# Masked attention with a residual on one core: the last outputs reordered, the short row group in four blocks, the seventh batch finished earlier

## The chip, the core and the metric

The kernel runs on one core of a Trainium2 chip. The engines of that core are TensorE (called PE in the profile, with its weight loads as PEld), VectorE (DVE), ScalarE (ACT), GpSimd (POOL) and SyncE (SP), and sixteen DMA engines move data between the memory outside (DRAM) and the core. Each engine works through its own list of instructions in order and waits at an instruction until what that one needs is there. The metric is the device time of one execution in microseconds; a lower one is better.

## The reference

`x` has the shape (8, 512, 1024): 8 batches, 512 features, 1024 tokens. For each batch the reference computes

```python
xt = jnp.transpose(x, (0, 2, 1))
q = xt @ Wq.T                                   # queries, keys and values are the same
qh = q.reshape(B, T, 8, 64).transpose(0, 2, 1, 3)
scores = jnp.einsum('bhqd,bhkd->bhqk', qh, qh) / 8
logits = (scores * cmask + (1 - cmask) * -1e30) * rmask
ctx = jnp.einsum('bhqk,bhkd->bhqd', jax.nn.softmax(logits, -1), qh)
x = x + jnp.transpose(ctx.transpose(...).reshape(B, T, D) @ Wo.T, (0, 2, 1))
```

The mask is 0 or 1 per token, about half and half. A masked token is no key for the others, and as a query it attends to all tokens evenly. So the kernel computes attention for the kept tokens alone, and one mean for all the rest.

## The kernel before, in words

For each batch the kept tokens are gathered to the front: 544 columns for the inputs at hand (`NK`), of which the last is the mean of the queries over all tokens and stands for the masked ones. These columns make five groups (`sizes`): four of 128, numbers 0 to 3, and a short one of 32, number 4, which the code calls `LAST`. The 512 features are four pairs of heads. A pair of a batch is the unit of the main loop in `late`: 32 pairs, four for each of the eight batches. I write (b, p) for the pair p of batch b; the last batch is 7 and the last pair (7, 3).

Each pair runs through five slots, one for each group c of keys. In a slot the kernel emits, in this order: the score products of the group (`scores`, L662, and L676 for the short group) and their exponentials on ACT (L685); the products of exponentials and values (`weigh_behind`, L709) of an earlier group; and then the tasks that `plan` has put into this slot. A task has a rank: those under 5 come first, then `contexts` of a pair that is due, then those from 5 up. The order is written out by hand and nothing is rearranged later, so a slot's place decides what stands ahead of what on each engine. PSUM has two buffers under the tag "t" for all the side products, two under "av", and two double ones for the scores.

What happens to a pair afterwards:

- `end_values` (L738) copies the weighted values to `cT`. `inverses` (L769 to L776, DVE) inverts the sums of the exponentials. For all but the last two pairs `invert` sends the inverses through DRAM to spread them over the partitions (`rb`). For the last two `spread` (L756) does it with 20 small products on PE and two copies on ACT (L763). In the kernel before, the spread for (7, 2) stands in slot 0 of (7, 3), right behind `inverses`.
- `contexts` (L803 to L812, DVE) finishes the inverses of the short group (`sum_last`), multiplies `cT` by `rb` and puts the mean into the last column.
- When all four pairs of a batch are done, `output` (L834) multiplies a group's contexts by the output weights, ACT copies the result (L841), and POOL's queue stores it to a table in DRAM, `od` (L846). The short group's output is computed in four blocks of 32 partitions and 128 columns.
- `load_rows` (L902, SP's queue) loads the rows of x, `fetch` (L943, POOL) gathers the rows of `od` and adds them in the DMA, `finish_blocks` (L913, DVE) turns 128 tokens of the result back to features by tokens in the tile `whole`, and `issue_stores` (L922, SP's queue) writes `whole` out, four stores for each half of batch 6 and of batch 5.

For the last batch there is another end. `begin_output` (L861) computes a group's output over the first three pairs and ACT copies this partial result (L869, `pa`); it runs in the slots of (7, 3). Behind the loop stand the last values' products, `spread` for (7, 3), the partial output of the short group, `sum_last`, `end_values_last` (L746, the contexts of the last pair straight from PSUM), and `end_output` (L876) for the groups 0, 4, 1, 2, 3: the product over the last pair, the sum with the partial result on DVE (L884) and the store on SP's queue (L885). Then DVE turns the last two token blocks of batch 6, SP's queue stores the second half of its `whole`, `fetch_last` (L934, POOL) gathers the rows of batch 7 by eight indirect DMAs, and `finish_tokens` turns each on PE (L960), adds x on DVE (L961) and stores on ACT's queue (L962). The first gather reads groups 0 and 4 alone, and each further gather one more group.

One more rule sets waits on PE: `note` remembers the first read of a PSUM buffer in a slot, and `open_slot` and `pass_gate` make the first value product (or crossed projection) of the next slot wait for it. Where no read was noted, it waits for the first exponential of the slot's own scores.

## Time and profile before

| | us |
|---|---|
| device time, median of 3 runs | 677.13 (675.56 to 678.43) |
| device time of the profiled execution | 679.92 |
| its span, first to last instruction | 677.9 |
| PE busy | 621.4 (92% of the span) |
| DVE busy | 362.0 (53%) |
| ACT busy | 360.5 (53%) |
| POOL busy | 184.1 (27%) |
| mean granted PE clock | 0.963 |

A row of the timeline gives the start, the duration, the engine, the line of the kernel, the operation, the tile written and the tile read, their shapes, how many records were merged (x16), and in brackets the idle time of the engine just before and what ended it. In the chain of work that ended last, a row is start, duration, what. In a table of stretches, each engine has its busy time, then come the granted PE clock, the share of the DMA engines that was busy, and GB/s. A product of 32-bit numbers leaves two records. SPq, ACTq and POOLq are the instructions that issue DMAs. The place of the tasks in this execution: (7, 0) runs from about 556 us, (7, 1) from 574, (7, 2) from 595, (7, 3) from 613, and the loop ends at about 639.

### The profile page before, as it was taken

Reading aid. Unit: us, or ns where it says so; the run is one execution under the profiler, and the core shown is the slowest. Engines: PE = TensorE matmul, PEld = TensorE weight load, DVE = VectorE, ACT = ScalarE, POOL = GpSimd, SP = SyncE. Lnnn points to the kernel's source line nnn. Section 1 sums busy time; section 2 is a strip of 40 time slices with the busy share of each in tenths; the row PEclk is TensorE's granted clock in tenths of the full one; section 3 lists DMA queues with packets and bytes.
Section 4 is the critical chain, followed back from the end, with each engine's and each line's share of the span. In section 5 each row is a group of like instructions: output and inputs, shape, how many; then the busy total and the mean of one; then the engine's idle time right before and its main releaser. Section 6 shows DMA issues by size and latency. Waiting matters only on the chain.

```text
span 677.9 us, 21834 instructions
## 1 busy us (share of the span) xinstructions
PE 621.4 (92%) x9056; PEld 413.2 (61%) x9056; DVE 362.0 (53%) x1113; ACT 360.5 (53%) x1010; POOL 184.1 (27%) x203
## 2 busy tenths in 40 slices
PE   6578989999999979999999999999999999998953
PEld 5345657677666656667666666676666655554422
DVE  6325885654564555555664566457645535234252
ACT  5127667656655645556656665656655445544300
POOL 4600221100134212341224304331334207006240
PEclk9688999999999989999999999999999999998985
DMA  8533663533366865696769777785857468744666
GB/s 277 170 122 98 197 192 89 165 97 113 103 197 141 215 185 154 205 252 164 198 227 247 169 187 247 195 196 150 233 135 144 130 212 154 211 146 78 128 197 190
DMA packets 98544, 117.10 MB, mean 173 GB/s; under 512 B 11785, under 2 KB 65625, under 8 KB 98426
## 3 DMA queue, kind: packets, MB, share of 16 engines
q1 hardware_dynamic: 77976, 75.71, 37.4%
q0 software_dynamic: 16224, 37.71, 24.4%
q10 hardware_dynamic: 4226, 2.10, 1.1%
q8 instruction: 75, 1.23, 0.8%
q14 instruction: 43, 0.35, 0.2%
HBM read 72.81 MB, written 42.67 MB: 170 GB/s over the span
## 4 chain that ended last, share of the span: by engine, by line
PE 76%; DMA 8%; DVE 7%; ACT 3%; SPq 2%; issue 2%; POOL 1%; DVEq 0%; ACTq 0%; POOLq 0%
PE s L662 17%; PE av L709 17%; PE pq L542 15%; PE po L834 15%; PE v L579 3%; DMA x<-in_x_dram 2%; PE pa L861 2%; PE xc L485 2%; DVE len L601 1%; ACT e L685 1%; DVE xc L488 1%; PE top L615 1%; PE s L676 1%; DMA rb<-row 1%; DMA g<-od,origin 1%
## 5 line engine op out<-in xcount | busy, mean ns | idle before, releaser
L685 ACT ACTIVATE e<-s,bias 128x544 f32<-128x544 f32 x256 | 180.3, 709 | 89.1 <-PE s L662 88.7
L709 PE MATMUL av<-e,v 64*64 64x272 f32 x2048 | 162.5, 398 | 7.9 <-ACT el L685 4.3
L662 PE MATMUL s<-qT 64*64 64x272 f32 x2048 | 155.8, 399 | 0.0
L542 PE MATMUL pq<-xc,wqT 64*64 64x272 f32 (+1 forms) x1984 | 127.5, 390 | 0.2 <-DVE xc L488 0.2
L709 PEld LDWEIGHTS av<-e,v 64*64 64x64 f32 x2048 | 85.5, 134 | 52.6 <-ACT cT L738 8.5
L834 PE MATMUL po<-woT,cT 128*128 128x256 f32 (+2 forms) x624 | 114.7, 363 | 0.0
L662 PEld LDWEIGHTS s<-qT 64*64 64x64 f32 x2048 | 82.3, 134 | 36.2 <-issue 6.9
L542 PEld LDWEIGHTS pq<-xc,wqT 64*64 64x64 f32 x1984 | 79.2, 134 | 37.5 <-issue 0.8
L943 POOL DMA_INDIRECT g<-od,origin x48 | 75.8, 1578 | 84.8 <-DMA g<-xd 60.5
L834 PEld LDWEIGHTS po<-woT,cT 128*128 128x128 f32 (+1 forms) x624 | 79.2, 164 | 28.8 <-issue 15.1
L846 POOL DMA_DIRECT2D od<-oc x56 | 31.3, 562 | 202.6 <-ACT oc L841 200.4
L472 POOL DMA_INDIRECT xin<-xd,source x40 | 39.8, 995 | 130.8 <-DMA row<-rt 71.8
L488 DVE COPY xc<-xc 128x512 f32<-128x512 f32 (+1 forms) x37 | 22.0, 613 | 61.4 <-PE xc L485 61.4
L559 DVE COPY qT<-pq 128x272 f32<-128x272 f32 x32 | 14.1, 439 | 70.2 <-PE pq L542 65.2
L841 ACT COPY oc<-po 128x256 f32<-128x256 f32 (+2 forms) x57 | 21.7, 382 | 55.8 <-PE po L834 55.8
L685 ACT ACTIVATION_READ_ACCUMULATOR e<-s,bias 128x1 f32 x256 | 50.2, 196 | 0.0
L588 DVE COPY v<-v 128x320 f32<-128x320 f32 x64 | 28.3, 483 | 34.3 <-PE v L579 34.3
L913 DVE STREAM_TRANSPOSE whole<-g 128x512 f32<-128x512 f32 x56 | 37.4, 687 | 13.8 <-DMA g<-od,origin 9.1
L601 DVE TENSOR_REDUCE len<-sq 128x10 f32<-128x640 f32 x32 | 26.1, 814 | 30.5 <-ACT sq L595 30.4
L738 ACT COPY cT<-av 128x272 f32<-128x272 f32 x62 | 21.1, 389 | 37.6 <-PE av L709 37.5
L425 ACT ACTIVATE junka<-x 128x512 f32<-128x512 f32 x64 | 40.2, 628 | 0.7
L462 DVE TENSOR_SCALAR_CACHE_REDUCE junk<-rank,key 128x1024 f32<-128x1024 f32 (+4 forms) x40 | 39.8, 996 | 0.0
(156 smaller groups left out, 633.4 us busy)
## 6 DMA issues: line engine op xcount, KB each, us to landing
xd<-xt SPq DMA_DIRECT2D x120, 128.0 KB
x<-in_x_dram SPq DMA_DIRECT2D x56, 256.0 KB
g<-xd SPq DMA_DIRECT2D x48, 256.0 KB
out_dram<-whole SPq DMA_DIRECT2D x20, 512.0 KB
rb<-row SPq DMA_DIRECT2D x60, 160.0 KB
od<-oc POOLq DMA_DIRECT2D x28, 256.0 KB
out_dram<-whole SPq DMA_DIRECT2D x16, 256.0 KB
rank<-ranks SPq DMA_DIRECT2D x7, 512.0 KB
```

The costliest lines, as they stand in the source:

```text
L425: nc.scalar.activation(junk, xs[b][r][:, d, :], AF.Copy, accum_out=xbars[b][:, d, r : r + 1])
L462: nc.vector.tensor_scalar(junk[:, :n], rank[:, i * P :], key[:, col], 0.0, ALU.is_le, ALU.add, accum_out=found[:, col])
L472: nc.gpsimd.indirect_dma_start(out=xin[:n, :], out_offset=None, in_=rows_of_x[b], in_offset=bass.IndirectOffsetOnAxis(ap=searches[b][2][:n ...
L542: mm = nc.tensor.matmul(pqs[pair][hf][heads[h], :n], wqT[rows, d, at : at + DK], xcs[b][rows, d, hf * KH : hf * KH + n], start=(not cross ...
L601: nc.vector.tensor_reduce(lengths, sq.rearrange("p c (h d) -> p (c h) d", h=2), axis=AX.X, op=ALU.add,)
L662: nc.tensor.matmul(s[h][to, hf, :KH], qT[heads[h], at : at + DK], qT[heads[h], hf * KH : (hf + 1) * KH], start=True, stop=True,)
L685: act = nc.scalar.activation(e[:, h], of[h], AF.Exp, bias=biases[pair][:, c : c + 1], scale=SCALE, accum_out=acc[:, h, c : c + 1],)
L709: mm = nc.tensor.matmul(avs[pair][hf][heads[h], :KH], v[rows, c, heads[h]], e[rows, h, hf, :] if c < LAST else e[rows, h, :], start=(c == ...
L834: nc.tensor.matmul(po[j * n : (j + 1) * n, cols], cTs[b, pr][:, i * P : i * P + n], woT[:, pr, j * w + cols.start : j * w + cols.stop], st ...
L846: nc.gpsimd.dma_start(od[places[i], j * w : (j + 1) * w], oc[j * n : (j + 1) * n, :w])
L913: nc.vector.transpose(whole.rearrange("p (d a) n -> p a d n", a=A)[:, :, :, i * Q : (i + 1) * Q], gs.pop((b, i)).rearrange("p (a d f) -> p ...
L943: nc.gpsimd.indirect_dma_start(out=gs[b, i], out_offset=None, in_=ods[b], in_offset=bass.IndirectOffsetOnAxis(ap=origin[:, b, i : i + 1] i ...
```

## The change

Five edits, all of them in the last two batches:

1. Batch 6's outputs of the groups 3 and 4 move from slot 3 of (7, 2) to (7, 1): the short one to slot 3, the other to slot 4. Its gathers move from slots (7, 2, 4) to (7, 3, 2) to slots (7, 2, 1) to (7, 3, 1), and its eight turns (`finish_blocks`), six of which stood in (7, 3) and two behind the loop, now stand in slots (7, 2, 4) to (7, 3, 4).
2. The spread for (7, 2) moves from slot 0 to slot 1 of (7, 3), and its copies on ACT are noted.
3. The partial outputs of batch 7: the short group's and group 0's in slot 2 of (7, 3), group 1's in slot 3, group 2's in slot 4, and group 3's behind the loop, behind the last values' products and the last spread. Before it was 0, 1, 2, 3 in slots 1 to 4 and the short one behind the loop.
4. The short group's partial and final products are made in four blocks of 32 partitions and 128 columns. Its sum is 128x128 where it was 32x512, and its store becomes four DMAs of 16 KB, two on ACT's queue and two on SP's. The final order is 0, 1, 4, 2, 3.
5. `end_values_last` multiplies the first half of the columns ahead of `sum_last`.

```diff
         for hf, av in enumerate(avs.pop(pair)):
+            if hf:
+                sum_last(pair)
             cols = slice(hf * KH, (hf + 1) * KH)
             nc.vector.tensor_tensor(cT[:, cols], av[:, :KH], rbs[pair][:, cols], ALU.mult)
...
-            nc.scalar.copy(rb[:, at * P : (at + n) * P], pt[:, : n * P])
+            note(nc.scalar.copy(rb[:, at * P : (at + n) * P], pt[:, : n * P]))
...
+    def last_products(b, i, prs, po):
+        n = max(Q, sizes[i])
+        for pr in prs:
+            first, last = pr == prs[0], pr == prs[-1]
+            if i < LAST:
+                to = po.rearrange("p (d a f) -> p d a f", a=A, d=ND)
+                nc.tensor.matmul(
+                    to, cTs[b, pr][:, i * P : i * P + n], plain(pr), start=first, stop=last
+                )
+                continue
+            w = D * n // P
+            for j in range(P // n):
+                nc.tensor.matmul(
+                    po[j * n : (j + 1) * n, :w].rearrange("p (d a f) -> p d a f", a=A, f=Q),
+                    cTs[b, pr][:, i * P : i * P + n],
+                    plain(pr)[:, j * (w // P) : (j + 1) * (w // P)],
+                    start=first,
+                    stop=last,
+                )
...
-        nc.vector.tensor_tensor(oc[:n, :], po[:n, :], partials[i][:n, :], ALU.add)
-        nc.sync.dma_start(od[places[i], :], oc[:n, :])
+        nc.vector.tensor_tensor(oc[:, :w], po[:, :w], partials[i][:, :w], ALU.add)
+        if i < LAST:
+            nc.sync.dma_start(od[places[i], :], oc)
+            return
+        for j in range(P // n):
+            (nc.scalar, nc.sync)[j % 2].dma_start(
+                od[places[i], j * w : (j + 1) * w], oc[j * n : j * n + sizes[i], :w]
+            )
...
+                put(nxt, 1, 3, output, b, LAST, 0, 1, rank=6.5)
                 put(nxt, 1, 4, output, b, 2, 0, 1, rank=6)
-                put(nxt, 2, 3, output, b, 3, 0, 1, rank=6)
-                put(nxt, 2, 3, output, b, LAST, 0, 1, rank=6.5)
+                put(nxt, 1, 4, output, b, 3, 0, 1, rank=6)
                 firsts = [(nxt, 1 + i // NC, i % NC) for i in range(NT)]
-                slots = [(nxt, 2, 4)] * 2 + [(nxt, 3, i // 2) for i in range(NT - 2)]
-                ends = [(nxt, 3, c) for c in (1, 1, 2, 2, 3, 3)]
+                slots = [(2, 1), (2, 1), (2, 2), (2, 3), (2, 4), (3, 0), (3, 0), (3, 1)]
+                slots = [(nxt, *at) for at in slots]
+                ends = [(2, 4), (2, 4), (3, 0), (3, 1), (3, 1), (3, 2), (3, 3), (3, 4)]
+                ends = [(nxt, *at) for at in ends]
...
-        for i in range(LAST):
-            put(last, 3, 1 + i, begin_output, last, i, rank=7)
+        for i, c in ((LAST, 2), (0, 2), (1, 3), (2, 4)):
+            put(last, 3, c, begin_output, last, i, rank=7)
...
-                if final and c == 0:
+                if final and c == 1:
                     spread(before, inv)
-                elif final and c == 1:
                     contexts(before)
...
-        begin_output(B - 1, LAST)
-        sum_last(last)
+        begin_output(B - 1, LAST - 1)
         end_values_last(last)
-        for j, i in enumerate((0, LAST, *range(1, LAST))):
+        for j, i in enumerate((0, 1, LAST, 2, 3)):
             end_output(B - 1, i, ("t", "av")[j % 2])
-        for i in range(NT - 2, NT):
-            finish_blocks(B - 2, i)
         while stores[0] or stores[1]:
             issue_stores()
```

The stores of the second half of batch 6's `whole` keep their place on SP's queue: behind the last batch's stores to `od`.

More of the change, by code (lines that the diff above doesn't have):

```diff
@@ L856, in begin_output, with width @@
+    def width(i):
+        return D * max(Q, sizes[i]) // P
     def begin_output(b, i):
-        n = sizes[i]
         po = bank(f"pa_{b}_{i}")
-        for pr in range(ND - 1):
-            nc.tensor.matmul(
-                as_plain(po[:n, :]),
-                cTs[b, pr][:, i * P : i * P + n],
-                plain(pr),
-                start=(pr == 0),
-                stop=(pr == ND - 2),
-            )
+        last_products(b, i, range(ND - 1), po)
         pa = sb.tile([P, D], F32, tag="xin", name=f"pa_{b}_{i}", bufs=NC)
-        note(nc.scalar.copy(pa[:n, :], po[:n, :]))
+        note(nc.scalar.copy(pa[:, : width(i)], po[:, : width(i)]))
@@ L870, in begin_output @@
         partials[i] = pa
     def end_output(b, i, tag):
[L873 removed]
+        n, w = max(Q, sizes[i]), width(i)
         od = place_outputs(b)
         po = bank(f"po_{b}_{i}", tag)
[L876 to L884 removed]
```

11 lines of the change are left out of this document (1 added, 10 removed).

## The prediction

> **What bounds the kernel now.** I read the page's parts 1 and 4 first, then the chain in order of time from 585 us on, then the timeline of the engines there, and last a table of stretches for the clock and the DMA share. The change touches nothing ahead of (7, 1), so only the last 100 us matter.
>
> ```profile
> PE 621.4 (92%) x9056; PEld 413.2 (61%) x9056; DVE 362.0 (53%) x1113; ACT 360.5 (53%) x1010; POOL 184.1 (27%) x203
> ```
>
> The chain of work that ended last (start, duration, what):
>
> ```profile
> 591.73 3.44 PE po L834 x8
> ...
> 606.90 4.64 PE po L834 x40
> ...
> 618.11 2.40 PE rb L756 x20
> ...
> 625.09 1.08 PE s L662 x16
> ...
> 627.09 2.77 PE pa L861 x6
> ...
> 642.75 2.76 PE pa L861 x6
> 645.51 4.82 PE po L876 x10
> 650.36 0.69 DVE oc L884
> ...
> 657.17 7.12 DMA g<-od,origin
> ...
> 667.39 0.69 DVE x L961
> ```
>
> PE carries the chain up to the last products at 645.5 to 650.3. Behind them come the stores to `od`, the gathers, the turns and the stores to the output. The stretches (busy us by engine, then granted clock, DMA share, GB/s) show what limits that end:
>
> ```profile
> 16.87:20.29 3.42, 1.51 (x56) 1.23 (x46) 3.30 (x17) 1.62 (x3) 0.00 (x0) 1.00 0.60 191
> 20.29:23.70 3.41, 0.24 (x8) 0.19 (x8) 1.56 (x12) 0.00 (x0) 1.52 (x2) 1.00 0.10 15
> 614.21:617.62 3.41, 1.17 (x22) 0.62 (x12) 2.93 (x11) 2.24 (x7) 1.43 (x1) 1.00 0.05 12
> 617.62:621.04 3.42, 2.93 (x28) 2.42 (x32) 0.47 (x4) 0.75 (x2) 2.81 (x3) 0.50 0.57 79
> 648.00:654.00 6.00, 2.59 (x7) 0.84 (x5) 4.51 (x12) 0.00 (x0) 2.54 (x3) 1.00 0.68 224
> 654.00:671.50 17.50, 8.32 (x32) 5.73 (x32) 5.53 (x8) 0.00 (x0) 5.09 (x6) 0.53 1.01 290
> 671.50:677.90 6.40, 0.00 (x0) 0.00 (x0) 0.00 (x0) 0.00 (x0) 0.00 (x0) 0.50 0.10 23
> ```
>
> From 654 to 671.5 the DMA engines are full (1.01); before that, from 648, 0.32 of 6 us, 1.9 us, is left unused. So the end is two things in a row: PE up to the last products, then the DMA engines. The 6.4 us behind 671.5 I leave as they are. I measure both against X, the start of the last products, which is 645.5 now. Two rows are about the clock: PE was busy 1.17 of 3.41 us (0.34) from 614.21 on, and in the next 3.42 us the clock was 0.50.
>
> **The sum is made against the profiled execution** (span 677.9, device time 679.92, so 2.0 around it). Its time is 2.8 above the median of 677.13; the change in us is taken over to the median.
>
> **Batch 6's outputs moved from (7, 2) to (7, 1): +1.0.** The work itself is the same: 3.44 for group 3 (the row of 591.73 is such a group) and 4.64 - 3.44 = 1.2 for the short one leave (7, 2) and lengthen (7, 1), so everything in (7, 2) up to slot 3 stands 4.64 later and nothing is saved. But those 4.64 us stood between the exponentials of slot 3 and slot 4, and hid ACT's lag. Timeline rows of this place, and of (7, 0), whose slot 3 has no output either:
>
> ```profile
> 605.71 0.71 ACT L685 ACTIVATE e<-s,bias 128x544 f32<-128x544 f32 x1 [0.92 <-PE s L662]
> ...
> 613.01 0.32 PE L615 MATMUL top<-ident,top 128*128 128x128 f32 x1
> ```
> ```profile
> 566.81 0.71 ACT L685 ACTIVATE e<-s,bias 128x544 f32<-128x544 f32 x1 [0.92 <-PE s L662]
> ...
> 569.46 1.15 PE L709 MATMUL av<-e,v 64*64 64x272 f32 x16 [1.00 <-ACT el L685]
> ...
> 570.53 0.32 PE L615 MATMUL top<-ident,top 128*128 128x128 f32 x1
> ```
>
> With no output noted, the first value product of slot 4 waits for the slot's own exponential (1.00 idle), and from the first exponential of slot 3 to the product `top` it is 3.72 us. In (7, 2) it is 7.30 now, less 4.64 makes 2.66. So 3.72 - 2.66 = 1.06 is lost: (7, 3) begins at 614.3 where it began at 613.26. In (7, 1) the two outputs follow others, their PSUM buffers are read by ACT while PE runs the next product: nothing is added.
>
> **The spread a slot later: -1.0.** The rows of slot 0 and 1 of (7, 3):
>
> ```profile
> 613.26 1.20 PE L662 MATMUL s<-qT 64*64 64x272 f32 x16
> ...
> 614.69 0.69 PE L709 MATMUL av<-el,v 64*64 64x272 f32 x8
> ...
> 617.88 0.12 DVE L776 COPY ris<-sums 128x2 f32<-128x2 f32 x1
> 618.11 2.40 PE L756 MATMUL rb<-ident,ris 128*64 128x128 f32 x20 [2.73 <-DVE ris L776]
> ...
> 620.91 0.23 DVE L803 TENSOR_TENSOR rb<-rb 128x64 f32<-128x64 f32 x1 [2.91 <-ACT rb L763]
> ...
> 622.25 0.72 DVE L811 TENSOR_TENSOR cT<-cT,rb 128x544 f32<-128x544 f32 x1
> ...
> 623.11 1.41 DVE L913 STREAM_TRANSPOSE whole<-g 128x512 f32<-128x512 f32 x2
> ...
> 640.97 1.31 PE L756 MATMUL rb<-ident,ris 128*64 128x128 f32 x20
> ```
>
> PE waits 2.73 us for DVE's inverses and then runs at half clock: the 20 products take 2.40 where the same take 1.31 at 640.97, and the scores behind them 0.15 to 0.3 more. Together this place costs 2.73 + 1.09 + 0.2 = 4.0. Afterwards the scores and value products of slot 1 fill part of the wait, but two turns of batch 6 (1.41) now stand on DVE ahead of the inverses. Counted from the start of (7, 3): PE is through with slot 1 at about 4.1 (0.3 of it waiting for slot 0's second exponential), and the inverses end at 618.00 - 613.26 + 1.41 = 6.15, so PE waits about 2.2 us. Then rb until 7.5, slot 2's scores and values (2.00, from 625.09 to 627.09) until 9.5. The short partial's products need the contexts of (7, 2): DVE takes 622.97 - 620.91 = 2.06 behind ACT's copies, which end at 8.2, so they come at 10.3 or a little later and PE waits some 0.55 (eight of the twelve products run in between). Waits after: 0.3 + 2.2 + 0.55 = 3.05, against 4.0. The noted copy on ACT ends 1.7 behind the start of rb (642.75 - 640.97 = 1.78 includes it), ahead of the value products that now wait for it (1.31 + 1.08 = 2.39 behind): nothing.
>
> Whether the clock falls in this new gap is the open cost. The rows above bound it: a stretch of 3.41 us with PE busy 0.34 of it lost the clock, one with 0.44 (1.51 of 3.42) kept it. The gap of 2.2 leaves 0.36 in a stretch that holds all of it and more in one that cuts it. I take it as kept; lost, it costs half of 3.41, of which some 0.6 falls into the wait for the contexts: +1.1.
>
> The Trainium skill (TensorE: Matmul & The Clock Gate, section "What's actually happening") says that the gate judges free-running windows of 4096 cycles at 1.2 GHz, 3413 ns; the half clock from 617.6 to 621.0 agrees. Its section "Why this matters for your kernels" allows idle gaps up to about 3 us; by that the 2.2 us gap is safe and the sum stays, but the trace lost the clock after 2.73.
>
> **Partial outputs reordered, the short one in blocks: -1.9.** The three slots keep one group of 2.8 each. Behind the loop the short group's 2.76 (642.75) becomes group 3's 2.76, and the short group moves into slot 2 with 12 products of 32x128: 12/16 of 1.2 is 0.9. So -2.76 + 0.9 = -1.86 ahead of X. Behind X the short final product falls from about 0.96 to 0.3, and its sum on DVE becomes shorter. `sum_last` between the halves of the contexts changes the order on DVE and not its end, which lies within group 3's 2.76.
>
> X moves by +1.06 - 0.95 - 1.86 = -1.75, to 643.7.
>
> **The end behind X: -0.7.** Rows of the queues:
>
> ```profile
> 612.16 1.98 POOL L846 DMA_DIRECT2D od<-oc  x4 [0.17 <-issue]
> ```
> ```profile
> 647.33 4.07 SPq L885 DMA_DIRECT2D od<-oc  x5
> ...
> 650.74 1.00 POOL L934 DMA_INDIRECT g<-od,origin  x1 [19.01 <-DVE oc L884]
> ...
> 652.29 14.43 SPq L922 DMA_DIRECT2D out_dram<-whole  x4
> ```
>
> The first gather starts 5.3 us behind X: 2.9 to the sum of the short group and 2.4 for its store. In the new order that sum ends at about X + 3.0 (third, but after products of 0.9, 0.9 and 0.3), so the gather starts where it did or a little later. The four stores pass nothing that is due on ACT's queue; on SP's they stand ahead of the stores of groups 2 and 3 by 0.7 us, which are not ready earlier. The four stores of batch 6's second half no longer wait for the two turns (they began 6.8 behind X) and follow the last `od` store at about X + 5.1, so 1.7 sooner; they can fill part of the 1.9 us of unused DMA time. What is left is bound by the same bytes. Bounds: 0, if the gathers stay the limit, and -1.9, if all of it is filled. I take -0.7, nearer the lower end, as the first gather does not move with them.
>
> Sum: 1.06 - 0.95 - 1.86 - 0.7 = -2.45. 677.13 - 2.5 = **674.6**.
>
> **The gathers of batch 6 earlier: 0.** They leave slots in which DVE waited for them; POOL has nothing else.
>
> ```profile
> 596.08 0.54 POOL L846 DMA_DIRECT2D od<-oc  x1 [4.92 <-ACT oc L841]
> ...
> 616.19 2.11 POOL L943 DMA_INDIRECT g<-od,origin  x1 [2.04 <-DVE rb L806]
> ...
> 620.50 1.53 POOL L943 DMA_INDIRECT g<-od,origin  x1 [0.30 <-issue]
> ```
> ```profile
> 627.02 0.71 DVE L913 STREAM_TRANSPOSE whole<-g 128x512 f32<-128x512 f32 x1 [2.50 <-DMA g<-od,origin]
> ```
>
> The last store to `od` is issued at 596.08 + 4.64 and done at 601.3, the first gather starts some 2.0 later and the second about 2.2 behind it, at 605.5; a gather lands 6.5 behind its start (620.50 to 627.02), so at 612. DVE wants it at about 618.7, behind the contexts of (7, 1). The cover is over 6 us.
>
> **The rivals.**
> - **The clock falls in the new gap.** For it: 2.2 idle is close to the 2.73 that lost it, and my 2.2 is a difference of estimates. Against: 0.44 kept it. It gives 674.6 + 1.1 = 675.7.
> - **The four small stores hold up the first gather.** The four of 612.16 took 1.98 to issue, and the gather behind them began at 616.19: 4.0 from the first issue, against 2.4 for the one store now. That would be +1.6, 676.2, if they went through one queue; against it, they go through two. The Trainium skill (DMA: Bandwidth & Descriptors, section "Rules for kernel authors") speaks against this edit too: it advises to coalesce small transfers, since under 64 KB mostly overhead is paid. The trace of before agrees only so far as the four on POOL's queue took 0.5 us each to issue.
> - **The end fills up altogether.** The unused 1.9 us all go: 677.13 - 1.75 - 1.9 = 673.5.
> - **Slower: the turns wait for their gathers.** DVE's two turns now stand ahead of the inverses for which PE waits. If the second gather lands behind 618.7, PE stands still for as long; behind 621.2 the gain is gone. For it: DVE did wait for gathers (2.50). Against: the cover of 6 us. A gather that lands at 624.5 would give 680.4.
>
> **How the numbers follow.** Forecast 0.44; clock lost 0.24; small stores 0.10; end filled 0.13; turns late 0.09. A measurement of this kernel can tell about 0.5%, 3.4 us, from no change (673.7 to 680.5). Faster than that are the filled end and the forecast's lower edge: 0.25. Slower is the last rival beyond 680.5, and what I have not seen in the rows: 0.09. Within: 0.66. The range runs from 672.4 (filled end, less the 1.1 by which a run falls below) to 678.2 (a gather late by 3.5 beyond its cover, or small stores with the clock lost and nothing filled). The forecast's own range is 673.6 to 675.6.
>
> **What would show it.** Right: a value-product wait of about 1.0 on ACT's `el` in (7, 2); PE idle near 2.2 ahead of rb with the clock at 1.00 behind it; 12 short products under 1 us; the last products about 29.4 behind the start of (7, 3), near 643.7; no wait on the gathers among DVE's turns; a fuller DMA share in the 6 us behind the first `od` store. Wrong: a clock of 0.50 behind rb, a wait of DVE for `g` in slot 4 of (7, 2), a first gather more than 5.8 behind X, or an end of the stores that does not follow X.

## The result and the profile after

The changed kernel takes 675.66 us (median of 20 runs, 672.26 to 677.68), the kernel before in the same comparison 677.15 us (20 runs, 675.56 to 680.69). The ratio is 0.9964, with a 95% interval of 0.9951 to 0.9978, so 1.5 to 3.3 us are gained; 2.4 in the middle, where 2.45 was forecast. The two medians as they stand differ by 1.5: 675.66 is 1.1 above the forecast of 674.6 and just above its own range of 673.6 to 675.6, inside the whole range of 672.4 to 678.2. The profiled execution took 675.11 us, its span is 673.4.

The experiments ran on other chips, on which the kernel before takes between 678 and 694 us; so what is compared is ratios, and stretches of the trace between the same points: the start of (7, 1), of (7, 2) and of (7, 3) (their first score products), X, and the end of the span. Already at the start of (7, 1) the two profiled executions differ by 2.2 us (574.22 and 572.00), which the change can't have caused. PE's busy time on the page of the changed kernel is 3.7 us less than the 621.4 of before:

```profile
PE 617.7 (92%) x9080; PEld 411.4 (61%) x9080; DVE 360.3 (54%) x1113; ACT 360.1 (53%) x1010; POOL 183.6 (27%) x203
```

The chain of work that ended last, in order of time:

```profile
590.24 6.87 PE po L836 x16
...
637.70 2.84 PE pa L862 x6
...
654.31 6.42 DMA g<-od,origin
```

Batch 6's outputs of the groups 2 and 3 now stand one behind the other at 590 (6.87 for the two), the last partial at 637.70 is group 3's, and behind X one gather stands on the chain as before, with 6.42 us where it was 7.12. The timeline of PE at the places that the prediction priced (start, duration, engine, line, operation; in brackets the idle time before and what ended it):

```profile
610.30 1.15 PE L709 MATMUL av<-e,v 64*64 64x272 f32 x16 [1.00 <-ACT el L685]
...
611.63 1.15 PE L662 MATMUL s<-qT 64*64 64x272 f32 x16
...
617.39 1.31 PE L758 MATMUL rb<-ident,ris 128*64 128x128 f32 x20 [1.37 <-DVE ris L778]
...
620.62 0.64 PE L868 MATMUL pa<-woT,cT 128*32 128x128 f32 x16
621.61 0.43 PE L868 MATMUL pa<-woT,cT 128*32 128x128 f32 x8 [0.34 <-DVE cT L814]
...
640.38 1.88 PE L862 MATMUL po<-woT,cT 128*128 128x512 f32 x4
```

The wait of 1.00 for `el` is there, PE is idle 1.37 ahead of `rb` and the 20 products behind take 1.31, so the clock stayed at full rate. The partial products of the short group (24 records) take 0.64 + 0.43 with 0.34 idle between. X is 640.38. The queues behind X:

```profile
642.16 1.20 SPq L895 DMA_DIRECT2D od<-oc  x2
...
643.22 0.79 ACTq L898 DMA_DIRECT2D od<-oc  x2
643.45 0.87 SPq L898 DMA_DIRECT2D od<-oc  x2
...
645.75 4.66 SPq L937 DMA_DIRECT2D out_dram<-whole  x4
...
646.73 1.00 POOL L949 DMA_INDIRECT g<-od,origin  x1 [28.25 <-DVE one L1390]
```

The `whole` stores of batch 6 start 5.4 behind X and are issued in 4.66 us instead of 14.43. The first gather starts 6.35 behind X, where it was 5.29: more than the 5.8 that the prediction named as a sign that it is wrong. The stretch from X to the end of the span as one row (length, busy us of PE, PEld, DVE, ACT, POOL, granted clock, DMA share, GB/s), in the kernel before:

```profile
645.45:677.90 32.45, 13.46 (x44) 7.29 (x43) 11.08 (x21) 0.57 (x1) 7.63 (x8) 0.65 0.69 203
```

and in the changed one:

```profile
640.38:673.40 33.02, 12.72 (x50) 7.28 (x48) 9.41 (x19) 0.59 (x1) 7.65 (x8) 0.61 0.69 199
```

In lengths of these stretches (each is the difference of two starts; the third line is worked out from the prediction's terms):

| | (7,1) to (7,3) | (7,3) to X | X to the end | (7,1) to the end |
|---|---|---|---|---|
| before | 39.04 | 32.19 | 32.45 | 103.68 |
| changed | 39.63 | 28.75 | 33.02 | 101.40 |
| predicted change | +1.06 | -2.81 | -0.70 | -2.45 |
| change | +0.59 | -3.44 | +0.57 | -2.28 |

The sum is as forecast, its terms are not: X came sooner than forecast, and the end behind it did not shrink, the prediction's other sign of being wrong. Of the kernel before there is this one profile, so how far its own stretches vary from one execution to the next is not shown.

The record shows one thing more about that last stretch. The DMA packets of the last stores of x end 26.74 behind X in the kernel before and 27.61 in the changed one. From there to the end of the span no engine is busy, and the DMA engines move almost nothing. These are the rows of this tail for the changed kernel and for experiment 1 below:

```profile
667.99:673.40 5.41, 0.00 (x0) 0.00 (x0) 0.00 (x0) 0.00 (x0) 0.00 (x0) 0.50 0.09 15
```

```profile
679.51:686.30 6.79, 0.00 (x0) 0.00 (x0) 0.00 (x0) 0.00 (x0) 0.00 (x0) 0.50 0.08 12
```

In the fourteen profiles the tail is 4.8 to 6.8 us long, and none of the edits is made there. So X to the end carries up to 2 us that say nothing on the edits, and from X to the end of the last store of x (X to the last data below) is the better measure.

### The profile page after: what moved, and what is told of

Same layout as the page of the kernel before. It is cut to its first block, busy times and chain, and to the rows that moved or that the text cites. A ratio compares the mean times of both kernels' runs of the same rounds, so it can differ in the third digit from the quotient of the medians.

```text
span 673.4 us, 21889 instructions
## 1 busy us (share of the span) xinstructions
PE 617.7 (92%) x9080; PEld 411.4 (61%) x9080; DVE 360.3 (54%) x1113; ACT 360.1 (53%) x1010; POOL 183.6 (27%) x203
## 4 chain that ended last, share of the span: by engine, by line
PE 68%; DMA 11%; DVE 9%; issue 5%; ACT 3%; SPq 1%; POOL 1%; DVEq 0%; POOLq 0%; ACTq 0%
PE s L662 15%; PE av L709 15%; PE po L836 14%; PE pq L542 14%; DMA x<-in_x_dram 4%; PE v L579 2%; PE xc L485 2%; DMA g<-od,origin 2%; PE pa L862 2%; DMA xd<-xt 2%; DVE len L601 1%; DMA row<-rt 1%; PE s L676 1%; PE top L615 1%; DVE junk L462 1%
## 5 line engine op out<-in xcount | busy, mean ns | idle before, releaser
L836 PEld LDWEIGHTS po<-woT,cT 128*128 128x128 f32 (+1 forms) x624 | 79.0, 163 | 28.5 <-issue 16.2
```

The costliest lines, as they stand in the source:

```text
L836: nc.tensor.matmul(po[j * n : (j + 1) * n, cols], cTs[b, pr][:, i * P : i * P + n], woT[:, pr, j * w + cols.start : j * w + cols.stop], st ...
```

## The experiments

The question is why nothing was gained behind X. One theory (G in the expectations) is that the first gather sets the end, and that it started later than before; the other (B, later V) that the bytes do, whatever their order. All edits are against the changed kernel, but for that of 11, which is against 9. The ratios of the single edits (0.9941 to 0.9951) and of the changed kernel (0.9964) have intervals that overlap, so what follows goes by stretches of one profiled execution each. Edit 5 and the noting of the spread's copies were not tried alone.

**1. The short output second.**

```diff
-        for j, i in enumerate((0, 1, LAST, 2, 3)):
+        for j, i in enumerate((0, LAST, 1, 2, 3)):
```

> The changed kernel with one edit: the final order is 0, 4, 1, 2, 3, as in the kernel before, with the four small stores kept. In the changed kernel the first gather starts 6.35 us behind the start of the last products (X) and 3.54 behind the short group's sum; in the kernel before it was 5.3 and 2.41. Theory Q: the small stores wait behind the 256 KB of group 1 on the same queue. Then the first gather starts some 2.4 to 2.6 behind the short sum, at about X + 4.6, and the stretch from X to the end falls from 33.0 to about 32. Rival S: the four small stores cost themselves, in issue and in completion. Then it stays near 3.5 behind the sum, at about X + 5.6, and the end at X + 32.5 to 33.

Ratio to the kernel before 0.9951 (0.9925 to 0.9977). X is 653.30. Its timeline at the first gather:

```profile
658.74 1.00 POOL L949 DMA_INDIRECT g<-od,origin  x1 [26.55 <-DVE worst L1385]
```

The last row of SP's queue, and then the stretch from X to the end:

```profile
673.82 0.32 SPq L937 DMA_DIRECT2D out_dram<-whole  x1
```

```profile
653.30:686.30 33.00, 11.12 (x50) 6.97 (x48) 9.40 (x19) 0.58 (x1) 7.64 (x8) 0.66 0.69 199
```

The gather starts 0.9 sooner, 5.44 behind X, and the end is still 33.00 behind it. It starts 3.5 behind the short sum, as the expectation has it for S. The last sum on DVE ended 21.3 behind X instead of 24.1, but the last `whole` store was issued only 20.5 behind X. So the first gather alone does not set the end of the span. That it brings nothing is not shown: X to the last data is 26.21, where the changed kernel's three executions (experiment 5) have 26.85 to 27.61, and the tail of 6.8, the longest of all, took this back.

**2. Batch 6's second-half stores ahead of the last outputs' stores.**

```diff
         end_values_last(last)
+        while stores[0] or stores[1]:
+            issue_stores(4)
         for j, i in enumerate((0, 1, LAST, 2, 3)):
```

> The changed kernel with one edit: the four stores of batch 6's second half stand ahead of the last batch's stores to od on SP's queue instead of behind them; their data is ready at 624.5 by the changed kernel's profile, 16 us ahead of X. Theory B (the end behind X is bound by the bytes that the DMA engines move): 1.05 MB leave it, at 290 GB/s 3.6 us, so X to the end falls from 33.0 to 29.4 to 30.5. Rival G (it is bound by the chain of gather, turn, sum and store, with the gathers issued 1.25 us apart): it falls by less than 1, to 32 or more.

Ratio 0.9948 (0.9918 to 0.9978). X is 658.95; all eight stores of batch 6 now leave SP's queue before it (SP's timeline, then the stretch from X to the end):

```profile
640.77 7.17 SPq L937 DMA_DIRECT2D out_dram<-whole  x8
```

```profile
658.95:690.60 31.65, 13.17 (x50) 7.21 (x48) 9.41 (x19) 0.59 (x1) 7.66 (x8) 0.64 0.58 174
```

With 1 MB less behind X the DMA share falls from 0.69 to 0.58, and X to the end is 31.65, with a first gather that is not sooner (6.56). The sign is that of B; the size, 1.4 against the first profile and 0.9 against the mean of 32.5 in experiment 5, is less than the 2.5 or more that B expected (30.5 or less). X to the last data is 25.41, 1.4 to 2.2 less than in the changed kernel. What then ends last is probably the chain of gathers, sums and stores of x, whose last sum ended 22.8 behind X; no run separates this.

**3. The two turns of slot 4 of (7, 2) behind the inverses.**

```diff
-                ends = [(2, 4), (2, 4), (3, 0), (3, 1), (3, 1), (3, 2), (3, 3), (3, 4)]
+                ends = [(3, 0), (3, 0), (3, 0), (3, 1), (3, 1), (3, 2), (3, 3), (3, 4)]
```

> The changed kernel with one edit: the first two turns of batch 6 move from slot 4 of (7, 2) to slot 0 of (7, 3), so on DVE they stand behind the inverses of (7, 2) instead of ahead of them. Theory: these 1.31 us are what PE waits for ahead of the spread; its wait there falls from 1.37 to about 0.1, and from the start of (7, 3) to X it takes 27.4 to 27.6 instead of 28.75. Rival: another wait takes its place (slot 1's value products, ACT's copies), and less than 0.5 is gained.

Ratio 0.9941 (0.9911 to 0.9970). PE's timeline, at the spread and at X:

```profile
631.05 1.31 PE L758 MATMUL rb<-ident,ris 128*64 128x128 f32 x20 [0.24 <-issue]
...
654.04 1.88 PE L862 MATMUL po<-woT,cT 128*128 128x512 f32 x4
```

(7, 3) starts at 626.27, so X is 27.77 behind it, 0.2 above the 27.4 to 27.6 expected: the two turns ahead of the inverses cost 1.0. X to the end is 32.76.

**4. Edit 1 undone** (batch 6's outputs, gathers and turns where the kernel before had them).

```diff
-                put(nxt, 1, 3, output, b, LAST, 0, 1, rank=6.5)
                 put(nxt, 1, 4, output, b, 2, 0, 1, rank=6)
-                put(nxt, 1, 4, output, b, 3, 0, 1, rank=6)
+                put(nxt, 2, 3, output, b, 3, 0, 1, rank=6)
+                put(nxt, 2, 3, output, b, LAST, 0, 1, rank=6.5)
...
+        for i in range(NT - 2, NT):
+            finish_blocks(B - 2, i)
         while stores[0] or stores[1]:
```

> The changed kernel with edit 1 undone: batch 6's outputs, gathers and turns as in the kernel before, the rest as changed. Theory: edit 1 costs time ahead of X. From the start of (7, 1) to that of (7, 3) it is 39.0 again instead of 39.6, the wait ahead of the spread falls from 1.37 to about 0.1, so from the start of (7, 1) to X it takes 66.3 to 66.8 instead of 68.4; behind X it takes 33 to 33.7, so the whole is 1 to 2 us faster than the changed kernel, about 673.5. Rival: edit 1 pays behind X, which grows by 1.5 or more (34.5 and up) when it is undone, so that the whole is no faster than the changed kernel.

Ratio 0.9944 (0.9915 to 0.9973). (7, 1) to (7, 3) is 39.04 again, to the hundredth; (7, 3) to X is 27.85; X to the end 33.37. So edit 1 costs time ahead of X: (7, 1) to X is 66.89, about what was expected, against 68.38 in the first profile and 68.86 in experiment 1, which is on the same chip and differs from the changed kernel behind X alone. So it costs 1.5 to 2.0. Behind X it gives back 0.35 against the first profile and 0.8 against the mean of experiment 5.

**5. The changed kernel a second and a third time** (the third as a single execution, on the chip of 9 and 10).

> The changed kernel once more, on the chip of the other experiments. The four runs so far that vary one thing each agree on this: from (7,1) to (7,3) 39.6 to 40.2 us, from (7,3) to X (the start of the last outputs' products) 28.8, from X to the span's end 32.8 to 33.0 however early the first gather is. Theory V (behind X the DMA's volume sets the end, so X to the end repeats within 0.3): 32.7 to 33.1, first gather at X + 6.3, first to last together 101.4 to 101.9 from (7,1). Rival (the 33.0 of the first profile was chance, and X to the end is 31.7, as the prediction had it): 31.5 to 32.2. The ratio to the kernel before 0.995 to 0.997 on either.

> The changed kernel a third time, for its clock behind the spread. In the first profile PE waited 1.37 ahead of rb and kept its clock (rb 1.31), in the second it waited 1.68 and lost it (rb 2.40, (7,3) to X 30.04 instead of 28.75). Phase theory (the clock goes by windows on a grid that runs through, and the same gap costs it or not by where it lies on the grid): either one of the two, with nothing between: rb 1.31 and (7,3) to X 28.7 to 28.9, or rb 2.2 to 2.4 and 29.9 to 30.1. Rival (the clock goes by the gap's length, 1.5 or so being the point): the clock is lost if and only if the wait is over 1.55. X to the end 32.4 to 33.1.

Ratio of the second 0.9964 (0.9938 to 0.9990). X to the end is 32.41 and 32.19, so with the first profile's 33.02 it is 32.5 in the mean, and varies by 0.8, more than V expected: 32.41 lies between V's values and the rival's, and 32.19 is just inside the rival's, so V's claim that the stretch repeats failed. Against the 32.45 of before it neither shrank nor grew. X to the last data is 26.85 and 27.37 (27.61 in the first), so 0.1 to 0.9 longer than before. In the second execution (7, 3) to X took 30.04, in the third 28.86. PE's timeline at the spread, of the second and then of the third:

```profile
631.93 2.40 PE L758 MATMUL rb<-ident,ris 128*64 128x128 f32 x20 [1.68 <-DVE ris L778]
```

```profile
617.12 1.31 PE L758 MATMUL rb<-ident,ris 128*64 128x128 f32 x20 [1.49 <-DVE ris L778]
```

PE waited 1.68 and came back at half clock (2.40), or 1.49 and kept it (1.31): the rival that the prediction gave 0.24 happens, in one of the six profiles that have this gap (the first, 1, 2, 8 and the third kept it), and costs 1.2. More on it in the last section.

**6. Edits of 1, 2 and 3 together.**

> Three edits in one: batch 6's second-half stores ahead of the last outputs' stores, the short output second, the first two turns behind the inverses. Theory V (volume): the 1 MB taken from behind X frees the DMA there, so now the first gather counts: first gather X + 5.4 (the order's 0.9), X to the end 30.5 to 31.0 instead of 32.8; (7,3) to X 27.8 (the turns' 1.0), (7,1) to (7,3) 39.9 to 40.2; together 98.1 to 99.0 from (7,1), 2.5 to 3.5 less than the changed kernel, a ratio to the kernel before of 0.990 to 0.992. Rival (the gathers' data stay slow beside the outputs' stores, so that the order brings nothing here either): X to the end 31.6, as with the stores alone. Rival (gains do not add, the end is the fixed chain behind the last gather): no better than the best of the three alone, 0.994.

686.98 us against 693.16, ratio 0.9924 (0.9897 to 0.9952). X is 652.87, 27.75 behind (7, 3). The stretch from X to the end, then POOL's first gather:

```profile
652.87:684.30 31.43, 12.93 (x50) 7.23 (x48) 9.42 (x19) 0.59 (x1) 7.66 (x8) 0.64 0.59 175
```

```profile
658.54 1.00 POOL L949 DMA_INDIRECT g<-od,origin  x1 [27.38 <-DVE worst L1387]
```

X to the end is 31.43, so the gather, 0.9 sooner than in 2, brings 0.2, and X to the last data is 25.38, as in 2. The first rival has it nearly right: the order is worth next to nothing here. From (7, 1) it is 99.59, more than the 98.1 to 99.0 that was expected.

**7. The old outputs with early stores and the order of 1.** As 4, with the last two turns and the stores placed ahead of the last values' division:

```diff
+        for i in range(NT - 2, NT):
+            finish_blocks(B - 2, i)
+        while stores[0] or stores[1]:
+            issue_stores(4)
         end_values_last(last)
```

> Batch 6's outputs and turns where the kernel before had them, the last two turns and the second-half stores just ahead of the last values' division, the short output second. Theory V and the gate theory (the wait for el in slot 4 of (7,2) is the whole price of moving the outputs): (7,1) to (7,3) 39.04, (7,3) to X 27.9, X to the end 30.5 to 31.3; 97.4 to 98.3 from (7,1), the fastest of all, a ratio of 0.988 to 0.992. Rival (the last two turns wait for their gathers, which land only about 24 us behind (7,3), and hold up the inverses or the last values' division on DVE): (7,3) to X 28.5 to 30, and no gain over the other combination. Rival (the 1 MB that starts only 3 us ahead of X is still in the DMA's queues when the last outputs' stores come): first gather behind X + 6.5 and X to the end 32 or more.

687.01 us, ratio 0.9913 (0.9876 to 0.9950), 100.07 from (7, 1). DVE's timeline at the seventh and eighth turn:

```profile
644.23 0.71 DVE L928 STREAM_TRANSPOSE whole<-g 128x512 f32<-128x512 f32 x1 [0.39 <-DMA g<-od,origin]
650.42 0.71 DVE L928 STREAM_TRANSPOSE whole<-g 128x512 f32<-128x512 f32 x1 [5.47 <-DMA g<-od,origin]
```

The eighth turn waited 5.47 for its gather, and the division of the last values behind it began at 651.06, 0.5 ahead of X (651.60), where in 4 it begins 2.7 ahead (651.84 for 654.53). So the last products wait for contexts in their turn: the first gather starts at X + 8.32, and X to the end is 33.00. The first rival had the mechanism, though the wait shows behind X and not ahead of it ((7, 3) to X is 28.03, where it had 28.5 or more); the second had the numbers behind X.

**8. Edit 4 undone in its blocks** (the short output in products of 512 columns with one store of 64 KB; order and places as changed), a single execution.

```diff
...
-            for j in range(P // n):
-                nc.tensor.matmul(
-                    po[j * n : (j + 1) * n, :w].rearrange("p (d a f) -> p d a f", a=A, f=Q),
+            to = po[:n, :].rearrange("p (d a f) -> p d a f", a=A, d=ND)
+            nc.tensor.matmul(
+                to, cTs[b, pr][:, i * P : i * P + n], plain(pr), start=first, stop=last
+            )
...
```

> The changed kernel with the short output undivided, as the kernel before had it: three products of 512 columns a partial and one 64 KB store instead of four blocks and four 16 KB stores; places and order as in the changed kernel. By the prediction's sum, the blocks' part: 12 partial products cost 2.76 instead of 0.9 or so in the stretch from (7,3) to X, which grows by 1.5 to 1.9, to 30.3 to 30.7. Theory S (small stores: the gather starts 2.4 behind the last small store's issue, and the blocks' four stores cost one more issue in front of it): the first gather starts 2.4 behind the short sum instead of 3.5, at X + 5.7 to 6.0. Theory V: X to the end stays at 32.5 to 33.3 all the same. Rival (the four small stores are what lengthened the end): X to the end 31.5 to 32.

(7, 3) to X is 30.34 (X 659.07), 1.5 longer than the changed kernel's 28.75 and 28.86 at full clock. The timeline of DVE's short sum and POOL's first gather:

```profile
661.96 0.68 DVE L883 TENSOR_TENSOR oc<-po,pa 32x512 f32<-32x512 f32 x1 [0.28 <-PE po L861]
...
665.06 1.00 POOL L933 DMA_INDIRECT g<-od,origin  x1 [29.25 <-DVE worst L1369]
```

The short sum ends at 662.64 and the gather starts 2.42 behind it, as in the kernel before (648.33 and 650.74). With four stores it was 3.54 behind (643.19 and 646.73), and 2.4 behind the end of the second small store's issue on SP's queue (644.32). So the four small stores delay the gather by 1.1, for which the prediction's rival had 1.6. Whether that costs time is open: X to the end is 31.83 here, as the rival had it, on a chip where the changed kernel has 32.41; but one kernel varies by 0.8, and X to the last data is 26.88, as in the changed kernel's second execution (26.85).

**9. The wait for `el` filled:** the combination of 1 and 2, and of edit 1 the short output alone put back to slot 3 of (7, 2), gathers and turns behind it.

```diff
-                put(nxt, 1, 3, output, b, LAST, 0, 1, rank=6.5)
+                put(nxt, 2, 3, output, b, LAST, 0, 1, rank=6.5)
...
-                slots = [(2, 1), (2, 1), (2, 2), (2, 3), (2, 4), (3, 0), (3, 0), (3, 1)]
+                slots = [(2, 4)] * 2 + [(3, 0)] * 3 + [(3, 1)] * 3
...
-                ends = [(2, 4), (2, 4), (3, 0), (3, 1), (3, 1), (3, 2), (3, 3), (3, 4)]
+                ends = [(3, 1), (3, 1), (3, 2), (3, 2), (3, 3), (3, 3), (3, 4), (3, 4)]
```

> The order and the early stores as in the combination of three, and batch 6's short output alone taken back to slot 3 of (7,2), its gathers and turns behind it (two turns each in slots 1 to 4 of (7,3), none ahead of the inverses). Gate theory (PE's wait for el in slot 4 of (7,2), 1.0 to 1.1 in the traces, is there because PE has nothing else in that slot): the short output's 32 products fill it, the wait for el falls under 0.3, (7,1) to (7,3) 39.0 to 39.4 instead of 40.1 (the mean of seven profiles that have the outputs moved). The turns stay out of the way: (7,3) to X 27.8 to 28.0, X to the end 31.4 to 31.7 as in the combination of three, and from (7,1) 98.3 to 99.0 (combination of three: 99.59), a ratio to the kernel before of 0.990 to 0.992. Rival (the last two turns wait for their gathers in slot 4 and hold up the last inverses, as they held up the last values' division in the other combination): (7,3) to X or X to the end 1 to 2 longer, 100 or more from (7,1).

675.54 us against 678.40, ratio 0.9955 (0.9924 to 0.9986). The wait for `el` is gone from the trace and (7, 1) to (7, 3) is 38.85, less than the 39.04 of before: some 1 us of other work in that slot is worth 0.8 on this chip, where the changed kernel's third execution has 39.63. But the rival's mechanism came too, as PE's timeline at the last spread and DVE's at the eighth turn show:

```profile
639.42 1.31 PE L758 MATMUL rb<-ident,ris 128*64 128x128 f32 x20 [2.11 <-DVE ris L778]
```

```profile
637.87 0.71 DVE L928 STREAM_TRANSPOSE whole<-g 128x512 f32<-128x512 f32 x1 [2.20 <-DMA g<-od,origin]
```

The eighth turn waited 2.20 for its gather with the last inverses behind it, and PE 2.11 for those: (7, 3) to X is 30.01, 1.2 more than there. X to the end is 30.23 and X to the last data 24.27, the shortest of all; from (7, 1) it is 99.09, 1.6 less than the third execution and just above what the theory had (98.3 to 99.0).

**10. The spread back in slot 0 of (7, 3)**, a single execution.

```diff
-                if final and c == 1:
+                if final and c == 0:
                     spread(before, inv)
+                elif final and c == 1:
                     contexts(before)
```

> The changed kernel with the spread back in slot 0 of (7,3), the rest as changed. The prediction's sum priced the move at 0.95: (7,3) to X 28.8 + 0.95 = 29.8. Clock theory (the gap ahead of rb is what costs the clock, and slot 1's scores in front of it both shorten the gap by their 2.0 and keep the window busy): PE waits 3 to 4 us ahead of rb, as the two turns now stand in front of the inverses, the granted clock falls to 0.50 behind it, rb's 20 products take 2.2 to 2.4, and (7,3) to X is 30.8 to 32.5, so the move is worth 2 to 3.5 in the kernel as it is now. Rival (the gap is covered some other way): wait under 2, clock 1.00, 28.8.

PE's timeline at the spread, and two stretches of 3.41 us behind one another (columns as in the stretches above):

```profile
617.49 1.56 PE L758 MATMUL rb<-ident,ris 128*64 128x128 f32 x20 [3.77 <-DVE ris L778]
```

```profile
615.00:618.41 3.41, 0.92 (x17) 0.95 (x19) 2.85 (x10) 0.00 (x0) 2.80 (x3) 1.00 0.89 143
618.41:621.83 3.42, 3.42 (x32) 1.53 (x28) 2.21 (x7) 1.41 (x4) 1.07 (x1) 0.50 0.92 146
```

PE waits 3.77, the clock falls to 0.50 while rb's products run (they take 1.56, not the 2.2 to 2.4 expected), and (7, 3) to X is 33.06 where it is 28.86 on the same chip: the move is worth 4.2 in the kernel as it stands, more than the 2 to 3.5 expected. The two turns of edit 1 now stand in the same wait, which was 2.73 before.

**11. As 9, with the last two turns behind the last inverses.**

```diff
-                ends = [(3, 1), (3, 1), (3, 2), (3, 2), (3, 3), (3, 3), (3, 4), (3, 4)]
+                ends = [(3, 1), (3, 1), (3, 2), (3, 2), (3, 3), (3, 3)]
...
+        for i in range(NT - 2, NT):
+            finish_blocks(B - 2, i)
         while stores[0] or stores[1]:
             issue_stores(4)
         end_values_last(last)
```

> As the kernel that fills the wait for el, but batch 6's last two turns behind the last inverses instead of ahead of them, just ahead of the last values' division, and the second-half stores behind those turns. Theory (PE's wait of 2.11 for ris ahead of the last spread, in the profile of that kernel, is the two turns' waits for their gathers and nothing else): the wait goes, (7,3) to X falls from 30.01 to 27.7 to 28.0, and as the last gather had landed 24.0 behind (7,3) and the division starts 25.0 behind it, nothing new waits; (7,1) to (7,3) stays 38.85, X to the end 30.2 to 31.4; from (7,1) 96.8 to 98.3, against 100.7, 101.4 and 102.9 in the three profiles of the changed kernel; a ratio to the kernel before of 0.989 to 0.992. Rival (the stores now start 3 us ahead of X and their 1 MB is still in the queues when the last outputs' stores come, as in the combination with the old outputs): first gather X + 7 or later, X to the end 32 to 33, from (7,1) 99 to 100, a ratio of 0.993 to 0.996.

673.13 us against 678.10, ratio 0.9908 (0.9870 to 0.9945). The timeline of SP's queue, POOL and DVE at the eighth gather, and the stretch from X to the end:

```profile
625.55 4.87 SPq L937 DMA_DIRECT2D out_dram<-whole  x4
...
626.06 1.53 POOL L958 DMA_INDIRECT g<-od,origin  x1 [0.30 <-issue]
...
636.25 0.71 DVE L928 STREAM_TRANSPOSE whole<-g 128x512 f32<-128x512 f32 x1 [5.28 <-DMA g<-od,origin]
```

```profile
637.47:671.20 33.73, 13.06 (x50) 7.25 (x49) 10.96 (x24) 0.58 (x1) 7.65 (x8) 0.64 0.66 194
```

(7, 3) to X is 27.84 as expected. But the last gather, issued at 626.06 beside four stores of 256 KB, was there only at 636.25, 10.2 later (7.6 in 9), and the division of the last values waited for the turn behind it; the first gather of batch 7 starts at X + 8.30 and X to the end is 33.73. From (7, 1) it is 100.42. The rival's mechanism, then, by the trace, though the ratio is the lowest of all: the profile shows 3.3 us less than that of before, the times 3.7 to 8.8 less. Part of that lies ahead of (7, 1), which the edits do not touch: it starts at 570.78 here and at 574.22 in the kernel before. The rest is open.

## Why the prediction was right, and where it was not

By the prediction's own steps:

- **Batch 6's outputs, +1.06: the wait was right, the sum too large.** The wait of 1.00 stands where it was put, and (7, 2) became 3.56 shorter (18.16 to 14.60) where work of 4.64 had left it, so 1.08 is lost there. But (7, 1) became only 4.15 longer (20.88 to 25.03): 0.49 came back where the prediction put nothing. So (7, 1) to (7, 3) is 0.59 longer, 39.62 or 39.63, in the three profiles on chips where the kernel before takes 677 or 678. In six profiles on the slower chips it is 39.95 to 40.42, against 39.04 in all three with the outputs where they were; in five of the six another short wait stands in (7, 2). Experiment 9 shows that the wait is the cause, since short work there takes it away.
- **The spread, -0.95: right in its mechanism, mis-sized.** The wait was to be 2.2, it is 1.37 to 1.68, because the inverses end 5.65 behind (7, 3), not 6.15, and PE gets through slot 1 at 4.4, not 4.1. So the term measured about -1.9, twice its size: the -3.44 of the table less the 1.5 of the blocks (experiment 8). Turns and spread were priced in one term: the turns alone cost 1.0 (experiment 3), the move alone gains 4.2 (experiment 10).
- **Partials and blocks, -1.86: nearly right.** Undoing the blocks costs 1.5 ahead of X; the 24 records of the short partials take 1.07, not 0.9, and wait 0.34.
- **X, -1.75: too small.** (7, 1) to X shrank by 2.85 and 2.74 where the clock was kept and by 0.77 where it was lost. In the one profile of the kernel before the clock was lost at this place, too.
- **The end behind X, -0.7: this step failed.** It took part of the unused DMA time of the 6 us from 648 as a gain. That time was indeed filled: in the same 6 us, counted from X, the DMA share rose from 0.68 to 0.81, and from 3 to 24 us behind X from 0.93 to 0.96 (the stretch in the kernel before, then in the changed one).

```profile
648.45:669.45 21.00, 10.46 (x38) 6.37 (x36) 9.71 (x19) 0.00 (x0) 7.63 (x8) 0.66 0.93 273
```

```profile
643.38:664.38 21.00, 9.72 (x36) 6.07 (x34) 7.71 (x16) 0.00 (x0) 7.65 (x8) 0.60 0.96 281
```

- But X to the end, 33.02, 32.41 and 32.19, did not follow, and X to the last data is 27.61, 26.85 and 27.37, where it was 26.74. The `whole` stores went in ahead of the gathers, and these delivered later: the first one's rows were used 5.8 behind its start (652.49 for 646.73), before 4.3 (655.05 for 650.74); in the five profiles in which those stores stand ahead of the last outputs' stores (2, 6, 7, 9 and 11) it is 3.4 to 3.7. And the last sum of x ended 24.1, 23.5 and 23.3 behind X, not 22.6. What shortened the end was fewer bytes: in eleven of the fourteen profiles 6.5 to 6.6 MB move behind X (22.2 to 23.3 us of DMA time, the DMA share times the stretch), X to the last data is 26.2 to 27.6 and X to the end 31.8 to 33.7; in the three in which 1 MB had gone ahead (2, 6 and 9; 18.1 to 18.5) they are 24.3 to 25.4 and 30.2 to 31.7. The gather's delay of 1.06, which the prediction allowed for as "a little later" and its rival priced at 1.6, was real. Whether it cost part of what the stores gained is open: X to the last data was shorter with the sooner gather in 1, not in 6 or 8.
- **Gathers of batch 6 earlier, 0: right.** No turn of batch 6 waited for one in the first two executions of the changed kernel; in the third the last turn waited 0.29, with X where it was. Experiments 7, 9 and 11 show what the cover is worth: placed later, the eighth gather held up DVE by 2.2 to 5.5.

So that the total came out so near is luck: in the first profile the outputs cost 0.47 less than forecast and (7, 3) to X gained 0.63 more, while the end behind X came out 1.27 longer than forecast. Where the clock was lost, in the second execution, (7, 1) to the end is 102.87, 0.81 less than before.

Shorter than the changed kernel's three profiles (100.68 to 102.87 from (7, 1)) by over 1 us are 6 (99.59) and 9 (99.09). By the times 6, 7 and 11 have the lowest ratios, 0.9924, 0.9913 and 0.9908 against 0.9964; the intervals of 7 and 11 end just below that of the first measurement of the changed kernel, that of 6 touches it. That there is a faster version is likely by both; which of them is the best these runs do not tell.

## What to carry to other kernels

Where the end of a kernel is full of transfers, starting one of them sooner or reordering them gave little here (a gather 0.9 us sooner brought between nothing and 1.4 us up to the last data); taking 1 MB ahead of that stretch, into a time when the DMA engines have little to do, brought more (here the 15 us ahead of X, with a DMA share of 0.43, 0.00 and 0.01 in stretches of 5 us). And before stretches are compared up to the end of a span, look at what moves in its last microseconds: here a tail without any work varied by 2 us. Work that seems to be merely moved may have been the cover of another engine's lag: look at what stood between producer and consumer before, and leave there a piece that is just as long as the lag. And when a task that waits for a DMA is moved, look at what stands behind it on its in-order engine: the same kind of turn cost nothing, 1.0 or about 2 us, by what stood behind it.

## What the runs showed of the hardware

**The same gap costs the clock or not.** The falls and returns of the granted clock lie on one grid of 3.41 us in each run, so each run's stretches can be cut along it (length, PE busy, granted clock, DMA share, GB/s). The changed kernel's second execution, in which the clock fell behind the gap of 1.68:

```profile
628.36:631.77 3.41, 1.87 (x24) 1.00 0.93 147
631.77:635.19 3.42, 3.25 (x28) 0.50 0.94 153
```

its third, with a gap of 1.49:

```profile
614.37:617.79 3.42, 1.93 (x32) 1.00 0.91 140
617.79:621.20 3.41, 3.21 (x60) 1.00 0.85 126
```

and experiment 9 at its last spread, with a gap of 2.11:

```profile
634.97:638.39 3.42, 1.67 (x18) 1.00 0.99 220
638.39:641.80 3.41, 1.92 (x22) 1.00 0.59 147
```

A stretch with PE busy 1.87 of 3.41 (0.55) was followed by half clock, one with 1.93 (0.56) was not, and one with 1.67 (0.49) was not either; in experiment 10 and in the kernel before, 0.92 and 1.17 (0.27 and 0.34) were. So the length alone does not decide (2.11 kept the clock, 1.68 lost it), which takes away the rival of the expectation, and the busy share of one stretch does not either, which takes away the bound of 0.44 on which the prediction rested. Over whole runs it is the same: cut along its grid, each of the fourteen lost the clock behind every full-rate stretch with PE busy under 0.43, and between 0.43 and 0.75 some stretches lost it and some kept it. Where the gap lies on the grid may be what counts, as the one that lost the clock reaches over its stretch's end and that of 1.49 does not; but that of 2.11 does too, and the rule is open. What is shown is that a gap of 1.4 to 1.7 us, much the same in each execution, cost 1.2 us in one of six, so it can be a source of the scatter. The Trainium skill (TensorE: Matmul & The Clock Gate, "What's actually happening") describes free-running windows of 3413 ns, and the traces agree. Its section "Why this matters for your kernels" has idle gaps of up to about 3 us as safe; here 1.68 was enough to lose the clock.

**A gather behind large stores.** A gather of 256 KB that was issued together with four stores of 256 KB took 10.2 us to arrive in experiment 11, where it took 7.6 in experiment 9. The Trainium skill (DMA: Bandwidth & Descriptors, section on queues, rings and completion order) says that each DMA engine takes turns between the queues that have work; that agrees with a gather that slows down rather than waits for the stores' end, though no run here separates the two.
